# Winograd products of a gated FFN on one NeuronCore: another order of the second-level stages, and the last add and product of three units in four moved into the next unit

## The chip, the cores and the metric

The kernel runs on one core of one Trainium2 chip. The metric is the device time of one execution in microseconds. The engines are TensorE (PE; PEld for its weight loads), VectorE (DVE), ScalarE (ACT), GpSimd (POOL) and SyncE (SP). Each works through its own instructions in order, and they wait for one another by semaphores. TensorE writes its products to banks of PSUM.

## The reference

x has 4096 rows (2 x 2048) of 512 float32 values. Everything is float32.

```
x = x + attention(layernorm(x))     # scores and softmax over features (512 x 512), per batch
n = layernorm(x)
gate = n @ lut[gate_idx].T          # 4096 x 1376
up   = n @ lut[up_idx].T            # 4096 x 1376
h = silu(gate) * up
out = x + h @ lut[down_idx].T       # 4096 x 512
```

The table lut has 16 values; the index matrices have 1376 x 512 entries (down_idx 512 x 1376).

## The kernel before

**Stages.** Up to about 290 us of the profile the kernel does the first layernorm, the attention and the second layernorm. Then come the gate and up products (to about 815 us), then the down product. While TensorE multiplies, VectorE turns indices into weights: for each block of 128 rows of a weight matrix a chain of bit operations and predicated copies (`Job.ops`, lines 261 to 296). These lookups are traced in small portions between the stages of a unit: `between()` calls `pump(pace)`, which traces lookup operations worth about `pace` us.

**Units.** The 1376 hidden features are 11 blocks f (0 to 10; the last has 96), the 4096 rows are 4 pairs p of two chunks of 512. A unit (f, p), class `GateUp`, multiplies one block's gate and up weights with one pair of chunks. Gate and up, and two halves of the 512 features, make a 2 x 2 block product in Winograd's form, with 7 products instead of 8. Each is a stage of a unit that works on PSUM banks a, b and c (two of each in turn):

- a1 ("11"): bank a. ScalarE copies it to p1 (bank b in role 0, SBUF else).
- c1 ("S3","T3"): bank c. ScalarE copies it to p7, and in roles 2 and 3 also to v.
- a2 ("S2","T2"): added onto bank a. ScalarE copies the sum to u2.
- c2 ("22","T4") and b ("12","21"): see below.
- a3 ("S1","T1"): added onto bank a. VectorE makes c22 = a + p7.
- a4 ("S4","22"): added onto bank a. ScalarE makes h1 = silu(a). This stage runs inside the next unit, and so does `end`: h1 *= c22, stored to DRAM.
- `first`: h0 *= u2, stored to DRAM, where h0 is the silu of what b gives.

**Second level.** For f = 2 to 9 the stages b and c2 are done by Winograd once more, over 2 x 2 units: blocks f, f+1 and pairs p, p+1. Two objects of class `Second` do it: `of_b` (bank x, one only) and `of_c` (bank z, one only). Of the eight single products that b (or c2) of four units would take, each object saves one. A unit's place in the group is its role: 0 (f even, p even), 1 (f even, p odd), 2 (f odd, p even), 3 (f odd, p odd). The order of units is (f,0) to (f,3), so roles run 0 1 0 1 and, a block later, 2 3 2 3. Counting single products of 128x128 weights with 128x512 values: role 0 has 14, role 1 has 16, role 2 has 14, role 3 has 10 (no b and no c2 at all).

Role 1 makes "parts": after the products (S2,T2) and (S1,T1) of each object, ScalarE copies the bank (`part`, "r6" and "r5"), and SyncE stores the copy to DRAM; the object's next product is added onto the same bank and so waits for the copy. Role 2 adds a further product onto r5 by an accumulating DMA from GpSimd. Roles 2 and 3 get their parts back by accumulating DMAs from GpSimd onto p1 (for b) and v (for c2): `add_part`. So in role 2: u2 += z, u2 += v, h0 = x + p1; in role 3 u2 += v, h0 = silu(p1).

**The order that is written out.** `Line.run` (lines 1139 to 1162 before the change) traces one unit: a1, extra0, c1, extra1, the last unit's a4, a2, extra2, c2, the last unit's `end`, then b and a3 (a3 and b in the very last), then `first`; a `between()` stands behind each stage. The engines' queues follow this order exactly. `loads` (line 984) issues, ahead of a unit, the reloads of the right-hand sums T1, T2, T4 that the unit after it needs, on SyncE. `sums_left` makes the left sums S1 to S4 of both objects (tiles lb, lc; 4 operations each of 128x128).

In the profile, a product's operation has the line of `mm` (L998), with the bank as output: `a_g`, `b_g`, `c_g`, `x_g`, `z_g`. Adds have L136, subtractions L133; ScalarE's copies: p1 L1035, p7 L1050, v L1053, u2 L1059, parts L944; silu h0 L1109, silu h1 L1127; h0 * u2 L1119, h1 * c22 L1130. Buffer numbers are left out of names, so p1 and p7 both show as `p`, h0 and h1 as `h`.

Of the kernel before, what the change touches and what calls it, by code (L numbers as in the profile page):

```python
# [67 lines left out]
def tile_attn_ffn(  # L68
# [66 lines left out]
    def add(dest, a, b):  # L135
        nc.vector.tensor_tensor(dest, a, b, ALU.add)  # L136


    class Norm:
# [32 lines left out]
        def first(self, block):  # L172

            self.xn = xnp.tile([P, KB, 2, P], F32, tag="xn", name=f"xn_{self.name}_0", bufs=2)
            x = block.rearrange("p (i e) -> p i e", i=KB)
            half = KB // 2
            self.rest(0, 1, lambda: nc.vector.tensor_scalar(  # L177
                self.xn[:, half:, 0, :], x[:, half:, :], self.mv[:, 0, 0:1], self.rstd[:, 0:1],
                ALU.subtract, ALU.mult,
            ))  # L180
            nc.scalar.activation(
                self.xn[:, :half, 0, :], x[:, :half, :], AF.Identity,
                bias=self.nmr[:, 0:1], scale=self.rstd[:, 0:1],
            )
# [200 lines left out]
    def step():  # L385

        while deferred and deferred[0][0]():
            cost = next(deferred[0][1], None)
            if cost is not None:
                return cost  # L390
            deferred.pop(0)
        return next(lookup, None)
# [76 lines left out]
    def left(t, name, order=("S2", "S4", "S1")):  # L469
        a11, a21 = t[:, 0:2, :H], t[:, 0:2, H:]  # L470
        a12, a22 = t[:, 2:4, :H], t[:, 2:4, H:]

        def s3():
            for tag in order:
                o.new(tag)
            sub(a21, a11, a21)
            o.update({"11": a11, "12": a12, "22": a22, "S3": a21})

        o = Operand(name, [
            s3, lambda: sub(o["S2"], a22, a21), lambda: sub(o["S4"], a12, o["S2"]),  # L480
            lambda: add(o["S1"], o["S2"], a11),
        ])
        return o
# [111 lines left out]
    class Square:  # L595
# [7 lines left out]
        def mm(self, ps, a, b, first):  # L603
            for m in range(2):
                for k in range(2):

                    nc.tensor.matmul(  # L607
                        ps[:, m, :], self.a[a][:, k, m * P : (m + 1) * P], self.b[b][:, k, :],
                        start=first and m == k == 0, stop=k == 1,
                        skip_group_check=not (first and m == 0),  # L610
                    )
# [23 lines left out]
        def c2(self):  # L635
            self.mm(self.v, "22", "T4", False)
            add(self.c21, self.v, self.c21)
# [54 lines left out]
    g = [g_ops[0], left(gs[1], "g_1")]  # L692
# [186 lines left out]
    class Second:  # L879
# [34 lines left out]
        def sums_left(self, f):  # L914

            pool = wgu if self is of_b else x2p
            t = pool.tile([P, 4, P], F32, tag=f"l{self.name}", name=f"l{self.name}_{f}", bufs=1)
            (a11, a12), (a21, a22) = self.weights(f), self.weights(f + 1)
            s1, s2, s3, s4 = (t[:, q, :] for q in range(4))
            self.left = {"22": a22, "S1": s1, "S2": s2, "S3": s3, "S4": s4}  # L920
            return [
                lambda: add(s1, a21, a22), lambda: sub(s2, s1, a11),
                lambda: sub(s3, a11, a21), lambda: sub(s4, a12, s2),
            ]
# [33 lines left out]
    def in_two(t):  # L958
        return t[:, 0, :], t[:, 1, :]

    of_b = Second("b", "x", lambda f: in_two(gw[f][:, 2:4, :]), lambda p: in_two(xs[p]["21"]))
    of_c = Second("c", "z", lambda f: in_two(uw[f][:, 2:4, :]), lambda p: in_two(xs[p]["T4"]))
    seconds = [of_b, of_c]

    def there(f):
        return f in gw and len(gw[f].shape) == 3 and f in uw
# [17 lines left out]
    def loads(f, p):  # L984

        g = p // 2
        if 1 < f < NFT - 1 and f % 2 == 0 and p % 2:
            for tag in ("T2", "T1"):
                for o in (of_c, of_b):
                    o.load(g, tag)  # L990
        elif 1 < f < NFT - 1 and f % 2 and p % 2 == 0:
            for o in (of_c, of_b):
                o.load(g, "T4")
# [9 lines left out]
    class GateUp:  # L1003
# [57 lines left out]
        def c2(self):  # L1061
            if self.role is None:
                mm(self.c, self.pairs("22", "T4"), False)
                add(self.u2, self.c, self.u2)
            elif self.role == 0:
                of_c.begin(self, "11", "11")
                mm(self.c, of_c.pair(self, "12", "21"), False)
                add(self.u2, of_c.ps, self.u2)
                add(self.u2, self.c, self.u2)
            elif self.role == 1:  # L1070
                add(self.u2, self.c, self.u2)
                of_c.go_on(self, "S4", "22")
                add(self.u2, of_c.ps, self.u2)
            elif self.role == 2:
                of_c.go_on(self, "22", "T4")
                add(self.u2, of_c.ps, self.u2)
                add(self.u2, self.v, self.u2)

        def extra1(self):
            if self.role == 1:  # L1080
                of_c.go_on(self, "S1", "T1")
                of_c.part(self, "r5")
                of_b.go_on(self, "S2", "T2")
                of_b.part(self, "r6")
            elif self.role == 2:
                of_b.begin(self, "S3", "T3")
                of_b.part(self, "r5", onto=True)

        def extra2(self):
            if self.role == 1:  # L1090
                of_b.go_on(self, "S1", "T1")
                of_b.part(self, "r5")
# [21 lines left out]
            add(self.c22, self.a, self.p7)  # L1114

        def first(self):
            if self.role == 3:
                add(self.u2, self.v, self.u2)
            nc.vector.tensor_tensor(self.h0, self.h0, self.u2, ALU.mult)  # L1119
            self.store(self.h0, 2 * self.p)  # L1120
# [12 lines left out]
    class Line:  # L1133
# [3 lines left out]
            self.last, self.between = None, between  # L1137

        def run(self, u, final=False):
            u.a1()  # L1140
            self.between()
            u.extra0()
            u.c1()
            self.between()
            u.extra1()
            last, self.last = self.last, u
            if last is not None:
                last.a4()
                self.between()
            u.a2()  # L1150
            self.between()
            u.extra2()
            u.c2()
            if last is not None:
                last.end()
            self.between()
            one, two = (u.a3, u.b) if final else (u.b, u.a3)
            one()
            self.between()
            two()  # L1160
            u.first()
            self.between()

        def flush(self):
# [4 lines left out]
    pace = [1.0]  # L1169
# [93 lines left out]
    class Down:  # L1263
# [92 lines left out]
        def first(self):  # L1356
            pass

        extra0 = extra1 = extra2 = first

        def end(self):
            pass
# [3 lines left out]
    def by_two(ops):  # L1366
        return [
            lambda v=ops[i : i + 2]: [op() for op in v] for i in range(0, len(ops), 2)
        ]
# [5 lines left out]
    for (f, p), following in zip(units, units[1:] + [(NFT, 0)]):  # L1375
        while f not in gu or 1 < f < NFT - 1 and p and not there(f | 1):
            step()
        assert p in xs
        if 1 < f < NFT - 1 and f % 2 == 0 and p == 0:
            sums_of.append(f)  # L1380
        elif sums_of:
            for op in sums_left(sums_of.pop()):
                op()
        if f == NFT - 1 and p == 0:
            assert not todo and next(lookup, None) is None
            x2p.release()
            gub.release()
            for name in ("hp0", "dT"):
                hps[name] = tc.alloc_tile_pool(
                    name=name, bufs=1, side="right", reuse_waits="tile"  # L1390
                )
            hps[0] = hps["hp0"]
            h = Hidden(0)
            todo += by_two(sums_last(f) + down_sums(hps["dT"]))
        if f == NFT - 1 and p == 1:
            h.rest_of()
            todo += by_two(h.sums())
        if f == NFT - 1 and p == 3:
            units = [Down(h, 0)]
        loads(*following)  # L1400
        u = GateUp(f, p)
        pace[0] = {1: 1.2, 3: 0.8}.get(u.role, 1.07)
        line.run(u, final=(f, p) == (NFT - 1, NPR - 1))
        if p == NPR - 1:
            passed[0] = f + 1
        if (f, p) == (1, 1):
            xnp.release()
            x2p = tc.alloc_tile_pool(name="x2p", bufs=1, side="right", reuse_waits="tile")
        if f == 1 and p % 2:
            todo += by_two([op for o in seconds for op in o.sums(p // 2)])  # L1410
# [6 lines left out]
    for c in range(NCH):  # L1417
        nxt = None
        for jj in range(2):
# [10 lines left out]
            u = units.pop(0)  # L1430
# [64 lines left out]
```

## Time and profile before

| | us |
|---|---|
| median of 3 runs | 1091.05 |
| lowest, highest | 1088.09, 1091.49 |
| profiled execution | 1090.39 |
| its span | 1088.6 |
| TensorE busy | 1072.0 |
| VectorE busy | 768.7 |
| ScalarE busy | 360.4 |
| GpSimd busy | 79.7 |

The span is from the first to the last instruction of the profiled execution; its own time is 1.8 us more. TensorE's records overlap: two products in a row on one bank show as four records (each float32 product as two) of together 1.88 us, and the next stage starts 1.72 us after them. A number in brackets behind a row is the time that the engine stood idle before it, with what ended it. Row names hold engine, line, operation, output and inputs, shape and count.

### The profile page before, as it was taken

The numbers are of one execution on the slowest core, as the hardware profiler recorded it, in microseconds if no ns is written. First come the engines' busy times: TensorE is split into PE (matmuls) and PEld (weight loads), VectorE is DVE, ScalarE is ACT, GpSimd is POOL, SyncE is SP. The second block draws the span as 40 slices with busy tenths as digits, with TensorE's granted clock in tenths as the row PEclk, the third lists the DMA queues.
The fourth block names the chain that finished last, engine by engine and source line by source line (L and its number), as shares of the span: only waits on it lengthen the run. The fifth ranks groups of instructions, "written<-read, shape, count | busy, mean of one in ns | idle before, by whom it ended". The sixth has DMA issues, their size and how long they took to land.

```text
span 1088.6 us, 10783 instructions
## 1 busy us (share of the span) xinstructions
PE 1072.0 (98%) x3426; PEld 640.0 (59%) x3426; DVE 768.7 (71%) x1660; ACT 360.4 (33%) x671; POOL 79.7 (7%) x118
## 2 busy tenths in 40 slices
PE   9999999999999999999999999999999999999998
PEld 5668886444444444444434443444338888888887
DVE  7888777889885988898888888887543334433341
ACT  4652522554622233433443343333221111111110
POOL 0000000012110000310120031012000000000000
PEclk9999999999999999999999999999999999999999
DMA  8750314598651354653573466356515544345521
GB/s 343 227 164 22 76 40 97 141 226 215 175 142 39 118 181 155 156 144 136 145 161 131 163 143 148 130 144 143 158 53 172 172 152 156 98 148 178 156 68 39
DMA packets 107769, 153.89 MB, mean 141 GB/s; under 512 B 16432, under 2 KB 52528, under 8 KB 106816
## 3 DMA queue, kind: packets, MB, share of 16 engines
q1 hardware_dynamic: 75744, 107.51, 30.6%
q0 software_dynamic: 11904, 28.91, 13.4%
q10 hardware_dynamic: 20064, 16.78, 4.8%
q8 instruction: 27, 0.44, 0.2%
q14 instruction: 30, 0.25, 0.1%
HBM read 89.73 MB, written 63.44 MB: 141 GB/s over the span
## 4 chain that ended last, share of the span: by engine, by line
PE 86%; DVE 4%; DMA 4%; issue 3%; ACT 2%; POOL 1%; ACTq 0%; SPq 0%; POOLq 0%; DVEq 0%
PE a_g L998 22%; PE a_d L998 14%; PE y L770 10%; PE c_g L998 8%; PE c_d L998 7%; PE gp L454 4%; PE b_d L998 4%; PE z_g L998 3%; PE x_g L998 3%; PE b_g L998 3%; DMA v<-part_r_c 2%; PE ea_t L607 1%; PE ea_p L607 1%; PE ea_m L607 1%; DMA hd<-h 1%
## 5 line engine op out<-in xcount | busy, mean ns | idle before, releaser
L770 PE MATMUL y<-m,nT 128*128 128x512 f32 x256 | 110.2, 592 | 0.0
L998 PE MATMUL a_g<-xb,s 128*128 128x512 f32 (+1 forms) x176 | 83.2, 595 | 3.3 <-DVE c L136 3.3
L998 PE MATMUL a_g<-xT_a,s 128*128 128x512 f32 (+1 forms) x176 | 83.1, 594 | 2.7 <-ACT u L1059 2.7
L770 PEld LDWEIGHTS y<-m,nT 128*128 128x128 f32 x256 | 48.6, 190 | 60.4 <-issue 57.4
L998 PE MATMUL a_g<-xb,wg 128*128 128x512 f32 (+1 forms) x176 | 82.7, 592 | 0.0
L998 PE MATMUL c_g<-xb,wu 128*128 128x512 f32 (+1 forms) x176 | 82.7, 592 | 0.0
L454 PE MATMUL gp<-xn_a 128*128 128x128 f32 (+3 forms) x256 | 70.1, 434 | 1.5 <-DVE xn_a L177 1.2
L998 PE MATMUL a_g<-xT_sq,s 128*128 128x512 f32 (+1 forms) x132 | 62.4, 595 | 2.7 <-ACT u L1059 2.7
L998 PEld LDWEIGHTS a_g<-xb,s 128*128 128x128 f32 (+1 forms) x176 | 32.6, 187 | 47.6 <-issue 35.3
L454 PEld LDWEIGHTS gp<-xn_a 128*128 128x128 f32 x256 | 43.9, 190 | 28.3 <-issue 15.1
L998 PEld LDWEIGHTS a_g<-xT_a,s 128*128 128x128 f32 (+1 forms) x176 | 32.7, 187 | 46.6 <-issue 39.9
L998 PEld LDWEIGHTS c_g<-xb,wu 128*128 128x128 f32 (+1 forms) x176 | 33.0, 188 | 42.5 <-issue 42.3
L998 PEld LDWEIGHTS a_g<-xb,wg 128*128 128x128 f32 (+1 forms) x176 | 33.0, 188 | 42.5 <-issue 42.3
L290 DVE COPY_PREDICATED wd<-b_wd,wd 128x512 f32<-128x512 int16 (+1 forms) x77 | 56.5, 734 | 1.9
L998 PE MATMUL a_d<-dT,hs_a 128*128 128x256 f32 x224 | 56.2, 378 | 0.0
L136 DVE TENSOR_TENSOR u<-c_g,u 128x512 f32<-128x512 f32 (+1 forms) x28 | 19.3, 690 | 46.9 <-PE c_g L998 31.7
L136 DVE TENSOR_TENSOR r<-r,a_d 128x256 f32<-128x256 f32 x32 | 13.5, 421 | 53.7 <-PE a_d L998 53.7
L998 PEld LDWEIGHTS a_d<-dT,hs_a 128*128 128x128 f32 x224 | 42.4, 189 | 6.0
L998 PEld LDWEIGHTS a_g<-xT_sq,s 128*128 128x128 f32 (+1 forms) x132 | 24.4, 187 | 36.0 <-issue 29.5
L278 DVE TENSOR_SCALAR wd<-idx_wd,lut_x,lut_sb 128x512 int32<-128x512 int32 (+1 forms) x88 | 45.0, 540 | 0.0
L1109 ACT ACTIVATE h<-h 128x512 f32<-128x512 f32 x24 | 15.1, 631 | 84.8 <-DVE h L136 84.8
L1059 ACT COPY u<-a_g 128x512 f32<-128x512 f32 (+1 forms) x44 | 25.7, 585 | 46.7 <-PE a_g L998 42.8
(316 smaller groups left out, 2033.4 us busy)
## 6 DMA issues: line engine op xcount, KB each, us to landing
hd<-h SPq DMA_DIRECT2D x80, 256.0 KB, 2.0
h<-hd SPq DMA_DIRECT2D x40, 512.0 KB, 6.7
nl<-nd SPq DMA_DIRECT2D x32, 256.0 KB, 5.8
xnd<-xn_f ACTq DMA_DIRECT2D x16, 512.0 KB, 6.0
fl<-xnd POOLq DMA_DIRECT2D x32, 256.0 KB, 6.6
xn_back<-xnd SPq DMA_DIRECT2D x32, 256.0 KB, 4.2
out_dram<-r SPq DMA_DIRECT2D x31, 256.0 KB, 2.9
x<-in_x_dram SPq DMA_DIRECT2D x7, 1024.0 KB, 13.8
```

Source lines behind the costliest of these rows:

```text
L136: nc.vector.tensor_tensor(dest, a, b, ALU.add)
L278: vec.tensor_scalar(dest.bitcast(I32), idx, lut_x[:rows, k : k + 1], lut_i[:rows, at : at + 1], ALU.bitwise_and, ALU.bitwise_xor,)
L290: vec.copy_predicated(dest, masks[level - 1], t)
L454: nc.tensor.matmul(gp[b][i][:, i * P :], xn[:, i, j % 2, :], xn[:, i:, j % 2, :], start=c % CPB == 0 and j == 0, stop=c % CPB == CPB - 1 a ...
L607: nc.tensor.matmul(ps[:, m, :], self.a[a][:, k, m * P : (m + 1) * P], self.b[b][:, k, :], start=first and m == k == 0, stop=k == 1, skip_g ...
L770: nc.tensor.matmul(ys[k], nTs[k][:, i, :], m[:, i, :], start=(i == 0), stop=(i == KB - 1))
L998: nc.tensor.matmul(ps, lhsT, rhs, start=first and i == 0, stop=i == len(pairs) - 1, skip_group_check=not first,)
L1059: nc.scalar.copy(self.u2, self.a)
L1109: nc.scalar.activation(h0, self.p1 if self.role in (None, 3) else h0, AF.Silu)
```

## The change

1. Second-level stages of role 1: x of (S2,T2) goes from behind c1 (`extra1`) to behind a2 (`extra2`); x of (S1,T1) goes from there to behind c2 (a new `extra3`); a3 comes ahead of b in roles 1 and 3.
2. Role 3: the a4 of the unit before goes from ahead of a2 to behind a2.
3. Roles 1, 2 and 3: `first` (h0 *= u2 and the store) is traced in the next unit, behind its a1. The add u2 += v of role 2 goes there too (role 3 had it in `first` already).
4. `seconds` lists of_c ahead of of_b, so right-hand sums and left sums are made for c first; `loads` takes T2 and T1 of c, then T2 and T1 of b.
5. The paces are 1.3, 1.03 and 0.75 for roles 1, 2, 3 (before 1.2, 1.07, 0.8); role 0 and all others keep 1.07.

```diff
-    seconds = [of_b, of_c]
+    seconds = [of_c, of_b]
...
-            for tag in ("T2", "T1"):
-                for o in (of_c, of_b):
-                    o.load(g, tag)
+            of_c.load(g, "T2", "T1")
+            of_b.load(g, "T2", "T1")
...
                 add(self.u2, of_c.ps, self.u2)
-                add(self.u2, self.v, self.u2)
...
                 of_c.go_on(self, "S1", "T1")
                 of_c.part(self, "r5")
-                of_b.go_on(self, "S2", "T2")
-                of_b.part(self, "r6")
...
         def extra2(self):
+            if self.role == 1:
+                of_b.go_on(self, "S2", "T2")
+                of_b.part(self, "r6")
+
+        def extra3(self):
             if self.role == 1:
                 of_b.go_on(self, "S1", "T1")
                 of_b.part(self, "r5")
...
         def first(self):
-            if self.role == 3:
+            if self.role in (2, 3):
                 add(self.u2, self.v, self.u2)
...
         def run(self, u, final=False):
+            last, self.last = self.last, u
+
+            def last_a4():
+                if last is not None:
+                    last.a4()
+                    self.between()
+
+            role = getattr(u, "role", None)
             u.a1()
             self.between()
+            if getattr(last, "role", None):
+                last.first()
             u.extra0()
             u.c1()
             self.between()
             u.extra1()
-            last, self.last = self.last, u
-            if last is not None:
-                last.a4()
-                self.between()
+            if role != 3:
+                last_a4()
             u.a2()
             self.between()
+            if role == 3:
+                last_a4()
             u.extra2()
             u.c2()
             if last is not None:
                 last.end()
             self.between()
-            one, two = (u.a3, u.b) if final else (u.b, u.a3)
+            u.extra3()
+            one, two = (u.a3, u.b) if final or role in (1, 3) else (u.b, u.a3)
             one()
             self.between()
             two()
-            u.first()
+            if not role:
+                u.first()
             self.between()
...
-        pace[0] = {1: 1.2, 3: 0.8}.get(u.role, 1.07)
+        pace[0] = {1: 1.3, 2: 1.03, 3: 0.75}.get(u.role, 1.07)
```

More of the change, by code (lines that the diff above doesn't have):

```diff
@@ L1357, in first @@
             pass
-        extra0 = extra1 = extra2 = first
+        extra0 = extra1 = extra2 = extra3 = first
         def end(self):
```

## The prediction

> **What bounds the kernel now.** I read the page first, then TensorE's waits, then its timeline from 376 to 812 us, then VectorE, ScalarE and GpSimd (POOL) beside the places where TensorE stood. The page's first row:
>
> ```profile
> PE 1072.0 (98%) x3426; PEld 640.0 (59%) x3426; DVE 768.7 (71%) x1660; ACT 360.4 (33%) x671; POOL 79.7 (7%) x118
> ```
>
> The granted clock is full in every slice, so time can only be saved where TensorE stands still. The view of TensorE's waits names three kinds in the stage that is edited; all others lie before 130 us and are not touched:
>
> ```profile
> PE a_g L998 <- ACT u L1059: 5.4, 8, 0.7
> PE a_g L998 <- DVE c L136: 3.3, 4, 1.5
> PE z_g L998 <- DVE lc L133: 1.2, 1, 1.2
> ```
>
> A wait's number leaves out the tail and the restart, so I price waits by start to start. The edited stage (f = 2 to 9) runs from the a1 of unit (2,0) at 380.43 to the a1 of (10,0) at 765.54: 385.1 us. Eight groups of four units hold 14 + 16 + 14 + 10 = 54 products (unit kinds, "roles", 0 to 3), 432 in all. An undisturbed stage of two products takes 1.717 us start to start (443.89 to 445.61 below), so 432 need 370.9. **14.2 us are lost here**, and that is all that reordering can win. Where they go, in TensorE's timeline at a role-3 unit, (3,1):
>
> ```profile
> 443.89 1.88 PE L998 MATMUL a_g<-xT_sq,s 128*128 128x512 f32 x4
> 445.61 1.88 PE L998 MATMUL a_g<-xb,wg 128*128 128x512 f32 x4
> 447.32 1.88 PE L998 MATMUL c_g<-xb,wu 128*128 128x512 f32 x4
> 449.79 1.98 PE L998 MATMUL a_g<-xb,s 128*128 128x512 f32 x4 [0.58 <-DVE c L136]
> 451.61 1.88 PE L998 MATMUL a_g<-xT_a,s 128*128 128x512 f32 x4
> 454.16 1.98 PE L998 MATMUL a_g<-xT_a,s 128*128 128x512 f32 x4 [0.68 <-ACT u L1059]
> 455.98 1.88 PE L998 MATMUL a_g<-xb,wg 128*128 128x512 f32 x4
> ```
>
> The rows are a3 of role 2, then a1, c1, the a4 that belongs to role 2, a2, a3 of role 3, and the next a1. (i) a3 adds onto the bank that ScalarE must first copy out after a2, and role 3 has no product between: from 451.61 to 455.98 are 4.37 us for 3.43. 0.94 each, eight times: **7.5**. (ii) a4 adds onto the bank of role 2, which VectorE reads as c22; where that read is late a4 waits: 0.85 here, and by the same reckoning 0.22 at 544.76, 0.59 at 566.89, 1.18 at 641.29, 1.75 at 664.59: **4.6**. (iii) z at 395.50, once: **1.4**. (iv) **0.7**: eight times 0.08 in role 1. The sum is 14.2.
>
> Why c22 is late stands in VectorE's timeline:
>
> ```profile
> 443.30 0.69 DVE L136 TENSOR_TENSOR u<-z_g,u 128x512 f32<-128x512 f32 x1 [1.19 <-PE z_g L998]
> 445.05 0.69 DVE L136 TENSOR_TENSOR u<-v,u 128x512 f32<-128x512 f32 x1 [1.06 <-DMA v<-part_r_c]
> ...
> 447.33 0.69 DVE L136 TENSOR_TENSOR h<-x_g,p 128x512 f32<-128x512 f32 x1
> ...
> 449.05 0.69 DVE L136 TENSOR_TENSOR c<-a_g,p 128x512 f32<-128x512 f32 x1
> 449.65 0.68 DVE L1119 TENSOR_TENSOR h<-h,u 128x512 f32<-128x512 f32 x1
> ```
>
> VectorE works in order. u2 += v waits for a DMA that adds a part onto v, and h0 (h<-x_g) and c22 (c<-a_g) queue behind it.
>
> **The change, part by part.** No instruction is added or taken away on any engine; all of it is order.
>
> *a4 of role 2 goes behind a2 of role 3.* The 1.72 us of a4 then lie between a2 and a3, where ScalarE's copy costs 0.94: (i) goes, 7.5. a4 itself comes 1.72 us later, and the greatest lateness was 1.75; with the next part (ii) goes too, 4.6. What is late next: a3 now follows a4 at once, and the next unit's a1 takes the bank of a4, so ScalarE must finish silu(h1) within a3's 1.72 us; the product's tail of 0.16 and 0.60 for the silu (451.81) leave 0.9. a2 now follows c1 at once and needs the p1 copy (0.57) within c1: ScalarE made it 0.6 us late at 448.59 only because it sat behind silu(h0), which waited for the h0 add; that comes 1.1 us earlier below.
>
> *u2 += v and h0 * u2 of roles 1 to 3 go into the next unit behind a1; role 2's add no longer stands ahead of h0 and c22.* VectorE's wait for v in role 2 (1.06 here, up to 1.89 at 659.78) is gone: v landed from 0.5 us before to 0.3 us after the start of role 3, and the add now comes 3 to 4 us after it. The new wait: ScalarE's copy into v in role 3 needs this add, and behind that copy queue the u2 copy (which a3 needs) and silu(h1). From the rows of the tightest unit, role 2 at 647.49 and role 3 at 659.50: z add at 657.20, then h1 * c22 (0.60), two COPY_PREDICATED (1.4), h0 (0.60), two TENSOR_SCALAR (0.9), c22 (0.60), and three lookups (1.7 to 2.2), by the order of the changed program: the add begins 4.1 and ends 4.7 us behind role 3's a1. The v copy (0.59) then ends at 5.3 to 5.4, the u2 copy (0.58) at 6.0, and a3 is due at 6.9. In (7,1), where a cast of 0.5 stands between the copies, 6.5. No loss, with 0.4 to 0.9 us in hand. The price beyond that is one for one.
>
> Role 3's own add and product run in the next unit. The v DMA takes 5.5 us (3.9 to 6.7) and lands 10.6 to 11.8 behind role 3's a1; VectorE gets there at about 11 to 12. It may still stand 1 us, as now (0.48 at 457.50); c22 is already read, and the next v copy is due at 13.5. On SyncE the h0 store moves behind the next unit's loads, which so leave earlier; h0's buffer is written again some 9.5 us into that unit, and the store (2.0 us) ends by 6 or 7.
>
> *Role 1: x of (S2,T2) behind a2, x of (S1,T1) behind c2, a3 ahead of b.* Now one z product lies between the two x products, while ScalarE copies the part out. The same gap is there now, between (S1,T1) and (S4,22), in the timeline of the unit at 489.54:
>
> ```profile
> 498.99 1.02 PE L998 MATMUL x_g<-T_b_in,lb 128*128 128x512 f32 x2
> 499.84 1.02 PE L998 MATMUL z_g<-xT_a,lc 128*128 128x512 f32 x2
> 500.70 1.10 PE L998 MATMUL x_g<-xb,lb 128*128 128x512 f32 x2
> ```
>
> It costs the 0.08 of (iv). The old gap is filled by a3, the new one takes its place: (iv) stays, with bounds of -0.7 (both hidden) and +4 (a cast of 0.5 ahead of the copy, eight times; in the changed order none stands there). POOL and SyncE issue the same DMAs; the parts made in role 1 are read three units on, and r5 goes out behind an h1 store at no cost.
>
> *c before b in the left sums and the loads.* The lc sum that z at 395.50 waits for moves ahead of four lb operations (393.90 to 394.83): up to 0.93. But the next z needs the part's copy, which ScalarE ran at 397.49 to 398.08 behind a silu that waited for VectorE, and that z starts at 398.18, with or without the first. I take 0, with 0.93 as the other end. The loads only swap T1 of c with T2 of b, issued about 12 us ahead of use.
>
> *Pace.* 1.07 + 1.2 + 1.07 + 0.8 becomes 1.07 + 1.3 + 1.03 + 0.75: the lookups keep their rate. VectorE was 87 to 89% busy from 400 to 700 us; the same work in 373 instead of 385 us is about 91%, so it does not become the bound on the mean.
>
> **Sum.** 1090.39 (profiled execution: span 1088.6 and 1.8 around it) - 7.5 - 4.6 = **1078.3**. The median of the runs is 1091.05, 0.7 above, and they spread from 1088.09 to 1091.49. Below about 0.3% (3.3 us) a measurement of this kernel can't be told from no change.
>
> **The rivals.**
>
> *VectorE's lateness comes back through ScalarE.* The deferred add passes 4.8 us behind role 3's a1 in the crowded units, and the v copy holds the u2 copy. For it: 0.4 us of slack in (7,1), and a busier VectorE. Against it: its waits for z (1.0 to 1.5 in role 2) show that it catches up each unit. 7.5 saved, 4.6 given back elsewhere: 1082.9.
>
> *Role 3 is too short.* With a2 right behind c1 and a1 right behind a3, either waits as a3 did: 0.94 x 8 back, only 4.6 saved: 1085.8. Against it: 0.9 us of slack at the silu.
>
> *Nothing comes of it.* Both happen: 1090.4.
>
> *Slower: v lands late.* One place: the add of role 2's v, in role 3. TensorE loses once the add begins more than 4.8 us behind role 3's a1, that is, if v lands 4.5 us later than any did. At 7.0 in all eight units it would cost 8 x 2.2 = 17.6: 1095.9. For it: these DMAs are issued by POOL beside a VectorE that gets denser. Against it: POOL's issue of them took 861 to 1127 ns (median 870) at 89% VectorE busy, and the landings spread by only 2.8 us. The Trainium skill ("SBUF — State Buffer", "Who interferes with whom" and the box on SWDGE ahead of it) says that descriptors of POOL's DMAs wait while VectorE holds the port that both share, so by that rule denser work delays v. The issue times show at most a quarter of a microsecond of this, far from 4.5.
>
> **How the numbers follow.** The forecast 0.70, lateness through ScalarE 0.12, role 3 too short 0.06, nothing 0.07, slower 0.05. Faster by over 0.3% is the first three: 0.88. The range takes in the first two (0.82): below, 1078.3 - 0.9 - 0.7 and the 1 us by which runs differ, 1075.5; above, 1082.9 and the same, 1084.5.
>
> **What would show it.** Right: in TensorE's waits the eight "ACT u" are gone and the rows "DVE c" too; a role-3 unit takes 8.6 us from a1 to a1; (2,0) to (10,0) takes 373 us. VectorE's waits for v fall to those of role 3. Wrong: "ACT u" stays, now at an a3 behind a4, with the v copy late (rival one); a wait at a1 or a2 of or behind role 3 (rival two); v landing later than 7 us behind its issue (the slower one). The stages before 380 and behind 766 us should not change.

## The result, and the profile after

| | before | after |
|---|---|---|
| median of the runs, us | 1090.24 (4 runs, 1088.09 to 1091.49) | 1078.94 (4 runs, 1078.82 to 1079.50) |
| profiled execution, us | 1090.39 | 1078.93 |
| its span | 1088.6 | 1077.2 |
| TensorE from the a1 of (2,0) to the a1 of (10,0) | 380.43 to 765.54 = 385.11 | 380.47 to 754.09 = 373.62 |

The time after is 0.9899 of the time before, with a 95% interval from 0.9882 to 0.9917. Of the two profiled executions, the changed one is 11.46 us shorter, and its edited stage is 11.49 us shorter: outside that stage the two agree to 0.03 us in sum.

Lines from here on are those of the changed kernel (`mm` is L997, u2 copy L1058, v copy L1052, p1 copy L1034, silu of h1 L1128); kernels made from the one before keep its numbers (L998, L1059), and a run that adds or drops a line shifts them. The first row of the page of the changed kernel, and TensorE's waits in it from 380 to 770 us (sum, times, longest):

```profile
PE 1068.6 (99%) x3426; PEld 641.0 (60%) x3426; DVE 768.0 (71%) x1660; ACT 360.5 (33%) x671; POOL 79.7 (7%) x118
```

```profile
PE z_g L997 <- DVE lc L133: 0.9, 1, 0.9
PE z_g L997 <- ACT r_c L944: 0.7, 1, 0.7
```

The instruction counts are the same as before. The eight waits for the u2 copy and the four for c22 are gone, and the two rows that are left lie in one unit, the first of role 1. TensorE's timeline of the changed kernel at the role-3 unit (3,1):

```profile
444.58 1.88 PE L997 MATMUL a_g<-xT_sq,s 128*128 128x512 f32 x4
446.30 1.88 PE L997 MATMUL a_g<-xb,wg 128*128 128x512 f32 x4
448.01 1.88 PE L997 MATMUL c_g<-xb,wu 128*128 128x512 f32 x4
449.73 1.88 PE L997 MATMUL a_g<-xT_a,s 128*128 128x512 f32 x4
451.45 1.88 PE L997 MATMUL a_g<-xb,s 128*128 128x512 f32 x4
453.17 1.88 PE L997 MATMUL a_g<-xT_a,s 128*128 128x512 f32 x4
454.88 1.88 PE L997 MATMUL a_g<-xb,wg 128*128 128x512 f32 x4
```

Each stage starts 1.72 us behind the last, with no bracket. From a1 to a1 are 8.58 us, and a4 of role 2 (451.45) stands between a2 and a3. VectorE and then ScalarE beside it:

```profile
446.32 0.68 DVE L136 TENSOR_TENSOR h<-x_g,p 128x512 f32<-128x512 f32 x1
...
447.99 0.68 DVE L136 TENSOR_TENSOR c<-a_g,p 128x512 f32<-128x512 f32 x1
...
450.56 0.68 DVE L136 TENSOR_TENSOR u<-v,u 128x512 f32<-128x512 f32 x1
451.34 0.69 DVE L1120 TENSOR_TENSOR h<-h,u 128x512 f32<-128x512 f32 x1
```

```profile
448.21 0.59 ACT L1034 COPY p<-a_g 128x512 f32<-128x512 f32 x1 [0.55 <-PE a_g L997]
...
451.27 0.59 ACT L1052 COPY v<-c_g 128x512 f32<-128x512 f32 x1 [0.71 <-DVE u L136]
451.75 0.62 ACT L252 CAST b_u<-idx_u 128x512 int16<-128x512 int32 x1
452.27 0.59 ACT L1058 COPY u<-a_g 128x512 f32<-128x512 f32 x1
```

The adds to h0 and c22 now come first and wait for nothing. The deferred u2 += v begins 4.26 us behind a1. The v copy waits for it, a cast and the u2 copy follow, and that ends at 6.56, with a3 due at 6.87. The p1 copy here waits for TensorE alone.

By start to start, 2.8 us remain lost of 14.2: z in the first role-1 unit 2.14, and eight gaps of 0.08.

### The profile page after: what moved, and what is told of

The parts are those of the page before. It is cut to its first block, busy times and chain, and to the rows that moved or that the text cites. A ratio compares the mean times of both kernels' runs of the same rounds, so it can differ in the third digit from the quotient of the medians.

```text
span 1077.2 us, 10786 instructions
## 1 busy us (share of the span) xinstructions
PE 1068.6 (99%) x3426; PEld 641.0 (60%) x3426; DVE 768.0 (71%) x1660; ACT 360.5 (33%) x671; POOL 79.7 (7%) x118
## 4 chain that ended last, share of the span: by engine, by line
PE 90%; DVE 4%; ACT 2%; DMA 1%; issue 1%; ACTq 1%; SPq 0%; DVEq 0%
PE a_g L997 27%; PE a_d L997 14%; PE y L770 10%; PE c_g L997 9%; PE c_d L997 7%; PE b_d L997 4%; PE x_g L997 4%; PE z_g L997 4%; PE b_g L997 2%; PE ea_t L607 1%; PE ea_p L607 1%; PE ea_m L607 1%; DVE st_a L154 1%; PE gp L454 1%; DMA x<-in_x_dram 1%
## 5 line engine op out<-in xcount | busy, mean ns | idle before, releaser
L997 PE MATMUL a_g<-xb,s 128*128 128x512 f32 (+1 forms) x176 | 82.7, 592 | 0.0
L997 PE MATMUL a_g<-xb,wg 128*128 128x512 f32 (+1 forms) x176 | 82.7, 592 | 0.0
L997 PE MATMUL c_g<-xb,wu 128*128 128x512 f32 (+1 forms) x176 | 82.7, 592 | 0.0
L997 PE MATMUL a_g<-xT_a,s 128*128 128x512 f32 (+1 forms) x176 | 82.7, 592 | 0.0
L997 PE MATMUL a_g<-xT_sq,s 128*128 128x512 f32 (+1 forms) x132 | 62.0, 592 | 0.0
L997 PEld LDWEIGHTS a_g<-xb,s 128*128 128x128 f32 (+1 forms) x176 | 33.0, 188 | 42.5 <-issue 39.6
L997 PEld LDWEIGHTS a_g<-xT_a,s 128*128 128x128 f32 (+1 forms) x176 | 33.0, 188 | 42.5 <-issue 41.8
L997 PEld LDWEIGHTS c_g<-xb,wu 128*128 128x128 f32 (+1 forms) x176 | 33.0, 188 | 42.5 <-issue 42.3
L997 PEld LDWEIGHTS a_g<-xb,wg 128*128 128x128 f32 (+1 forms) x176 | 33.0, 188 | 42.5 <-issue 42.3
L997 PE MATMUL a_d<-dT,hs_a 128*128 128x256 f32 x224 | 56.2, 379 | 0.0
L997 PEld LDWEIGHTS a_d<-dT,hs_a 128*128 128x128 f32 x224 | 42.4, 189 | 6.0
L997 PEld LDWEIGHTS a_g<-xT_sq,s 128*128 128x128 f32 (+1 forms) x132 | 24.8, 188 | 31.9 <-issue 31.4
L1128 ACT ACTIVATE h<-a_g 128x512 f32<-128x512 f32 (+1 forms) x44 | 26.2, 597 | 43.9 <-PE a_g L997 43.9
```

The costliest lines, as they stand in the source:

```text
L997: nc.tensor.matmul(ps, lhsT, rhs, start=first and i == 0, stop=i == len(pairs) - 1, skip_group_check=not first,)
L1128: nc.scalar.activation(self.h1, self.a, AF.Silu)
```

## Experiments

The theory: (i) goes because a4 of role 2 covers the u2 copy; (ii) goes because a4 moves, and because VectorE no longer holds c22 and the p1 copy behind v; what is left is z. Rivals are named at each run. "Excess" is start to start less 1.717 us for two products, from each kernel's profiled execution. A ratio is to runs of the kernel before that were made beside the experiment (medians 1089.82 to 1090.42), with its 95% interval in square brackets.

**a4 back ahead of a2, the rest of the change kept.** In `run`:

```
-            if role != 3:
-                last_a4()
+            last_a4()
             u.a2()
             self.between()
-            if role == 3:
-                last_a4()
```

> The whole change but one part: the a4 of the unit before stays ahead of a2 in role 3. The theory (the a4 behind a2 is what hides ScalarE's copy ahead of a3) expects the eight waits of 0.94 us back and nothing else: 1078.9 + 7.5 = 1086.4 us, eight rows 'ACT u' of 0.68 us in TensorE's waits, and no row 'DVE c', since VectorE's read of c22 is no longer behind the wait for v. The rival, that a4 waits for c22 again as soon as it comes 1.72 us earlier, expects 1088 to 1091.

Measured 1086.76 (8 runs, 1084.93 to 1087.66), 0.9971 of before [0.9959, 0.9982]. TensorE's waits of this kernel:

```profile
PE a_g L997 <- ACT u L1058: 5.4, 8, 0.7
```

The row of before is back with all eight, at 0.7 each, and there is none for c22. The place of a4 alone is worth the 7.5 us of (i); without it the other edits still remove (ii).

**a4 behind a2 in role 3, nothing else changed from before.**

```
-            if last is not None:
-                last.a4()
-                self.between()
+            if role != 3:
+                last_a4()
             u.a2()
             self.between()
+            if role == 3:
+                last_a4()
```

> The kernel before with one part of the change: the a4 behind a2 in role 3. The theory: the eight waits of a3 (7.5 us) and the waits of a4 (4.6 us) both go, but a2 now follows c1 at once and needs the p1 copy, which ScalarE makes late behind a silu that waits for VectorE, which waits for v. By the rows of before, where p1 was copied 0.1 us (3,1), 0.6 us (7,1) and 2.0 us (7,3) behind the place of the new a2, some 3 us of waits at a2: 1081 to 1082 us. The rival, that the moved add of v brings nothing once a4 is moved, expects 1078.3.

Measured 1083.48 (3 runs, 1081.79 to 1084.36), 0.9934 [0.9903, 0.9965]. Its TensorE, VectorE and ScalarE at (3,1), whose a1 starts at 446.60:

```profile
448.32 1.88 PE L998 MATMUL c_g<-xb,wu 128*128 128x512 f32 x4
451.58 1.98 PE L998 MATMUL a_g<-xT_a,s 128*128 128x512 f32 x4 [1.38 <-ACT p L1035]
```

```profile
447.42 0.69 DVE L136 TENSOR_TENSOR u<-v,u 128x512 f32<-128x512 f32 x1 [2.43 <-DMA v<-part_r_c]
...
449.70 0.68 DVE L136 TENSOR_TENSOR h<-x_g,p 128x512 f32<-128x512 f32 x1
```

```profile
450.42 0.63 ACT L1109 ACTIVATE h<-h 128x512 f32<-128x512 f32 x1 [6.47 <-DVE h L136]
450.96 0.57 ACT L1035 COPY p<-a_g 128x512 f32<-128x512 f32 x1
```

To be read from below: a2 adds onto the bank that the p1 copy reads; the copy sits behind silu(h0); silu waits for the h0 add; that one is queued behind u2 += v, which waited 2.43 us for a DMA. No wait for the u2 copy or c22 is left, but a2 now loses 1.64 here and 5.1 in five of the eight units. So moving a4 alone saves (i) and (ii) and gives back 5.1, where about 3 was expected; z, too, lost 2.83 in this execution instead of 1.48. The deferral is what takes the p1 copy off that chain.

**The deferral alone, nothing else changed from before.** The add goes from `c2` of role 2 to `first`, and `first` of roles 1 to 3 goes behind the next unit's a1:

```
-                add(self.u2, self.v, self.u2)
...
-            if self.role == 3:
+            if self.role in (2, 3):
                 add(self.u2, self.v, self.u2)
...
             u.a1()
             self.between()
+            if getattr(last, "role", None):
+                last.first()
...
-            u.first()
+            if not getattr(u, "role", None):
+                u.first()
```

> The kernel before with one part of the change: u2 += v and h0 * u2 of roles 1 to 3 in the next unit. The theory expects the waits of a4 for c22 to go (4.6 us) and the eight of a3 to stay (7.5 us): 1085.8 us, no row 'DVE c', eight rows 'ACT u' of 0.68 us. The rival, that c22 is late because VectorE is busy and not because it waits for v, expects most of the 4.6 us to stay: 1088 to 1091.

Measured 1086.61 (7 runs, 1086.14 to 1086.86), 0.9971 [0.9959, 0.9983]. The waits for c22 are gone and all eight for the u2 copy stand (5.4 us in its row, as before). The deferral by itself is worth (ii); of the 0.8 us over the expectation 0.45 are z's (1.93 here, 1.48 before), and 0.4 lie outside the edited stage, which takes 380.96 us instead of 385.11.

**The x products of role 1 where they were**, a3 ahead of b kept: (S2,T2) of `of_b` goes from `extra2` back to `extra1`, (S1,T1) from `extra3` to `extra2`.

> The changed kernel, with the x products of role 1 where they were ((S2,T2) behind c1, (S1,T1) behind a2) and a3 ahead of b kept. Then a4 and a2, or z and a3, lie between any two x products. The theory expects the eight gaps of 0.08 us to go and nothing else to move: 0.7 us, 1078.2. The rival, that the new places of the x products carried a part of the gain, expects 1079.5 to 1082.

Measured 1078.19 (4 runs, 1077.31 to 1078.46), 0.9887 [0.9871, 0.9904]. The eight gaps of 0.08 are gone, and z lost 1.59 instead of 2.14. But a new wait of 0.34, 0.45 with its restart, stands at (7,1), where the add begins at 4.86. VectorE's row shows why:

```profile
631.70 0.69 DVE L136 TENSOR_TENSOR h<-x_g,p 128x512 f32<-128x512 f32 x1 [0.70 <-DMA hd<-h]
```

h0 of role 2 is written into the one buffer of h0, and the store of role 1's h0 had not landed. With (S2,T2) ahead of role 1's a2 again, VectorE reaches h0 * u2 0.9 us later; the store left 5.94 us ahead of the a1 of (7,1) instead of 6.89, and landed 0.48 behind it instead of 2.07 ahead. So the moved x products cost the 0.7 us of (iv), by the gaps that went, and kept this store out of the way. The 0.7 us between the two medians fit the expectation, but by the traces three terms add up to it: 0.67 of gaps and 0.55 of z gained, 0.45 lost.

**`of_b` ahead of `of_c` in the list again:** `seconds = [of_b, of_c]`.

> The changed kernel, with of_b ahead of of_c in the list again (the loads stay c first). The changed kernel lost 2.1 us at the two z products of the first unit of role 1, the kernel before 1.4 (one wait, and 0.05). The theory: VectorE's T sums stand still until a store to DRAM has freed their buffer, 3.6 us with c first and 2.9 with b first, and that sets both. It expects about 1.4 us here: 1078.2. The rival, that the order of c and b decides by its four operations, expects the first z wait to be 0.9 us longer than in the changed kernel: 1079.8.

Measured 1078.96 (4 runs, 1078.42 to 1081.29), 0.9900 [0.9886, 0.9915]. The profiled execution was the slowest, 1081.29; the other three lie beside the changed kernel's, so the times do not tell the two orders apart. In the profiled one 4.42 us are lost around the two z products, but not all of it by waiting. The granted clock was 0.5 from 397.39 to 400.80 us, while TensorE was busy, and full in the rest of the stage; the c1 between the two z's took 3.12 us instead of 1.88:

```profile
398.31 3.12 PE L997 MATMUL c_g<-xb,wu 128*128 128x512 f32 x4
```

3.41 us at half the clock cost 1.71; the waits lost the other 2.71. Beside the wait of VectorE's T sums for stores, in each execution with the three shared buffers:

| list | T sums wait, us | the two z's lose, us |
|---|---|---|
| c first (changed kernel 3.55) | 2.61, 2.75, 3.00, 3.55, 3.78 | 1.19, 1.34, 1.59, 2.14, 2.37 |
| b first (kernel before 2.88, this run 4.22) | 2.88, 3.35, 4.22, 4.28 | 1.48, 1.93, 2.71, 2.83 |

In both orders the loss is the wait less 1.4 to 1.5. So the theory's "that sets both" holds, but its 3.6 us for c first and 2.9 for b first were one execution each and not a property of the order. For the same wait, c first makes the first z lose 0.93 less and the second 0.93 more: the order is worth nothing.

**The store that z waits for.** The right sums T1, T2, T4 are made in three rotating buffers ("rt") and stored to DRAM; a fourth sum waits until the first is stored. Here those of `of_b`'s second pair get buffers that are free by then:

```
-                r[tag] = x2p.tile([P, CH], F32, tag="rt", name=f"{tag}_{self.name}{g}", bufs=3)
+                at, bufs = ("tt", 7) if self is of_b and g == 1 else ("rt", 3)
+                r[tag] = x2p.tile([P, CH], F32, tag=at, name=f"{tag}_{self.name}{g}", bufs=bufs)
```

> The changed kernel, with the T sums of b of the second pair of units in three buffers that are free at that time (those of the reloads), so that VectorE need not wait there for a store. The theory (the wait for the store sets the z products of the first unit of role 1) expects both z waits to go, 2.1 us: 1076.8. The rival, that the lc sums and the silu are late by VectorE's other work, expects at least 1 us to stay: 1078 or more.

Measured 1076.64 (4 runs, 1076.55 to 1076.93), 0.9875 [0.9861, 0.9890]. TensorE's timeline in the first role-1 unit, of the changed kernel and then of this one:

```profile
395.26 1.12 PE L997 MATMUL z_g<-T_c_in,lc 128*128 128x512 f32 x2 [0.90 <-DVE lc L133]
396.22 1.88 PE L997 MATMUL c_g<-xb,wu 128*128 128x512 f32 x4
398.82 1.13 PE L997 MATMUL z_g<-T_c_in,lc 128*128 128x512 f32 x2 [0.72 <-ACT r_c L944]
```

```profile
393.94 1.02 PE L998 MATMUL z_g<-T_c_in,lc 128*128 128x512 f32 x2
394.80 1.88 PE L998 MATMUL c_g<-xb,wu 128*128 128x512 f32 x4
396.52 1.02 PE L998 MATMUL z_g<-T_c_in,lc 128*128 128x512 f32 x2
```

Both brackets are gone, and the time falls by 2.3 us, about the 2.14 of z. The z wait comes from the three shared buffers, and so from the store that one of them waits for.

**The price of a late add, in two strengths.** Lookups are asked for ahead of the deferred add in role 3; the rate of role 3 is lowered to 0.6 (0.4 in the stronger):

```
             u.a1()
             self.between()
+            if role == 3:
+                pump(1.0)        # 2.5 in the stronger
             if getattr(last, "role", None):
                 last.first()
```

> The changed kernel, with 1 us more of lookups on VectorE ahead of the moved add in role 3 (and the pace of role 3 lowered from 0.75 to 0.6, so that the lookups keep about their rate). In the changed kernel the u2 copy ends 6.1 to 6.6 us behind role 3's a1 in the crowded units and a3 is due at 6.9. The theory of a slack of 0.3 to 0.8 us and a price of one for one beyond it expects the copy 1.0 to 1.4 us later, and so waits of a3 for 'ACT u' of 0.2 to 0.9 us in five or six of the eight units: 2 to 5 us, 1081 to 1084 us. The rival, that ScalarE's v copy is not on the path, expects 1078.9.

Measured 1079.48 (2 runs, 1078.68 and 1080.29), 0.9906 [0.9877, 0.9935]. The add moved by only 0.5 to 1.2 us in seven units, to begin at 4.2 to 4.85. The u2 copy ended at up to 7.00, and a3 was late in five units by 0.04 to 0.18 us (1.1 in all with the restarts). The 2 to 5 us that were expected did not come, and two runs are too few to tell the theories apart by time.

> The changed kernel, with 2.5 us of lookups asked for ahead of the deferred add in role 3 (the rate of role 3 lowered to 0.4, so that the lookups of a group stay about the same): 3 to 7 VectorE instructions more stand ahead of the add in seven of the eight role-3 units, some 0.57 us each. Theory (one for one beyond 4.8 us): the add begins at 5.5 to 6.8 us behind role 3's a1 in these seven, a3 waits for ScalarE's u2 copy by 0.8 to 2.0 us and 0.1 of restart in each, about 10 us in all, so 1087 to 1091. Rival (ScalarE's chain of add, v copy and u2 copy does not end on TensorE's path, and the small loss of the milder version was chance): no wait named for the u2 copy, 1079. Second rival (VectorE has idle time ahead of the add that takes up the lookups): the add begins below 5.3 us, under 3 us lost, 1080 to 1082.

Measured 1088.88 (10 runs, 1088.09 to 1090.22), 0.9981 [0.9971, 0.9990]. Its waits for the u2 copy, and ScalarE and TensorE at (3,1), whose a1 starts at 447.21:

```profile
PE a_g L997 <- ACT u L1058: 8.4, 7, 1.5
```

```profile
454.28 0.58 ACT L1052 COPY v<-c_g 128x512 f32<-128x512 f32 x1 [2.81 <-DVE u L136]
455.13 0.59 ACT L1058 COPY u<-a_g 128x512 f32<-128x512 f32 x1 [0.27 <-DVE h L1120]
```

```profile
455.77 1.55 PE L997 MATMUL a_g<-xT_a,s 128*128 128x512 f32 x3 [1.53 <-ACT u L1058]
```

In seven units the add begins at 5.7 to 6.4, and a3 is late in just these seven: 9.5 us, and 0.7 of restarts. In the six of them without a cast between the copies, a3 starts 2.14 to 2.21 us behind the start of the add. Added to 1078.94 the 10.2 us give 1089.1, and the median is 1088.88. The profiled execution itself took 1090.22: its edited stage is 9.45 longer than the changed kernel's (10.2, less 0.8 that z lost less), and the granted clock was 0.5 for 3.41 us from 7.89 us on, which cost 1.7 ahead of the stage. The chain from the add to a3 is on the path, and its price is one for one. The second bracket shows a link that the prediction did not have: the u2 copy also waits for h0 * u2, which reads the buffer that it writes.

**The best parts together:** the x products back and the free rooms.

> The changed kernel with both: x products of role 1 where they were, and free buffers for the T sums of b. If the two losses that are left (0.7 and 2.1 us) are as read, nothing is lost any more from the a1 of (2,0) to the a1 of (10,0): 370.9 us, and the time is 1078.9 - 2.8 = 1076.1. The rival, that they share a cause or that the next wait lies right behind, expects 1077 to 1079.

Measured 1076.19 (4 runs, 1076.03 to 1076.68), 0.9871 [0.9857, 0.9886]. One wait is left in the profiled execution, which was the slowest: 0.38 and a restart of 0.10 at (3,1), where the add began at 4.89. As in the run with the x products back, VectorE's add to h0 had waited for the h0 store there, by 0.55.

**And the deferred add ahead of the lookups behind a1, in role 3:**

```
             u.a1()
+            if role == 3:
+                last.first()
             self.between()
-            if getattr(last, "role", None):
+            if role != 3 and getattr(last, "role", None):
                 last.first()
```

> The last version (parts of x where they were, sums of b for the second pair in other rooms), and in role 3 the deferred add and product of role 2 stand directly behind a1, ahead of the lookups that follow a1: one lookup of 0.45 to 0.7 us fewer is queued ahead of the add. Theory (TensorE pays one for one for what the add begins beyond 4.8 us behind role 3's a1): the add, at 4.89 us in the crowded unit (3,1) of the last version, begins at about 4.2 to 4.4, ScalarE's u2 copy ends at 6.5 to 6.7, the wait of 0.38 with its restart of 0.10 there goes, and the time is 1075.7 (the last version measured 1076.19 median). No wait of TensorE is left between 380 and 766 us. Rival (the wait in (3,1) comes from the cast that stands between ScalarE's copies and not from the add): the wait stays and the time is 1076.2.

Measured 1076.27 (4 runs, 1076.24 to 1076.43), 0.9868 [0.9853, 0.9883]. In (3,1) the add begins at 3.49 and the u2 copy ends at 5.94, although the cast still stands there (4.68 to 5.30); the wait is gone, so it was the add's. The add came 1.4 us earlier, of which the edit explains 0.8: the h0 store landed 0.26 ahead of the add to h0, so that this one did not wait. No gap over 0.05 us is left, and from the a1 of (2,0) to that of (10,0) are 370.8 us. The time did not fall to 1075.7, though: that was reckoned from the median of the version before, whose profiled execution, the one with the wait, lay 0.5 above it. That is the 370.9 of an undisturbed stage: reordering can give no more in this stage.

## Why the prediction was right, point by point

**(i), 7.5 us: as said.** Gone in the changed kernel, back with a4 in its old place.

**(ii), 4.6 us: as said.** Either edit alone removes it. But the prediction's "a2 needs the p1 copy within c1", with the 1.1 us by which the h0 add comes earlier, turned out to be the reason that both are needed: with a4 moved alone, a2 pays 5.1. In the changed kernel the eight p1 copies begin 1.92 to 2.05 us behind a1 and a2 is due at 3.43. (The copy at 448.59 in the kernel before began 2.98 behind a1, so it was 1.06 late by this measure, not 0.6.)

**The new wait, ScalarE's v copy in role 3: no loss, as said; the slack was overrated by a little.** Forecast: the add begins at 4.1 us, the u2 copy ends at 6.0, or 6.5 with a cast. Measured in the eight units: 0.81 to 4.26, then 5.9 to 6.56. The add may begin no later than about 4.66 (6.87 less 2.21), not 4.8, since h0 * u2 stands between add and u2 copy; where a cast stands between the copies, a3 began 2.35 behind the add in three runs, and so no later than about 4.52. In the profiled execution of the changed kernel 0.3 us were in hand at the tightest place, (3,1), which has such a cast; (7,3), which the prediction took for the tightest, began its add at 3.92.

**z, taken as 0 out of 0 to 0.93: the order was worth the 0, and the term that was mis-sized is the wait behind it.** z's loss grew from 1.48 to 2.14, past both bounds. The lc sum moved ahead of four operations as expected, and the next z gave the 0.93 back as expected. But VectorE's T sums, ahead of both, wait for a store, and the prediction held that wait fixed. VectorE's wait in the kernel before, and then in the changed one:

```profile
388.69 0.69 DVE L133 TENSOR_TENSOR T_c<-xT_x,xT_sq 128x512 f32<-128x512 f32 x1 [2.88 <-DMA far_b1T<-T_b]
```

```profile
389.39 0.69 DVE L133 TENSOR_TENSOR T_b<-xb,xb 128x512 f32<-128x512 f32 x1 [3.55 <-DMA far_c1T<-T_c]
```

The store left 3.85 us behind the a1 of (2,0) in both and landed 5.05 us later instead of 4.37. These 0.67 us are the 0.66 by which z lost more, and the second z began at 398.82 and not at the 398.18 that the prediction gave it. Where it lands in one execution is luck as far as these runs go (see the last section), so the prediction's distance of 0.6 us from the result is, too. With the measured terms 1090.39 - 7.5 - 4.6 + 0.66 = 1078.95, and 1078.93 was measured.

**(iv), 0.7: stays, as said.** Eight gaps of 0.08, now at x's (S1,T1).

**The h0 store: later than reckoned, at no cost in the changed kernel.** The prediction let the store end 6 or 7 us into the next unit, ahead of a write at 9.5. In the changed kernel's units of role 0 it landed at 6.5 to 8.9, and the write came at 9.6. In role 3, where ScalarE's silu writes the buffer from 7.6 us on, it landed at 7.7 to 10.3 in seven of the eight units, and the silu stood for it by up to 2.67 us; TensorE did not wait for that silu. In role 2 VectorE's add to h0 waited for this store in two experiments, and there a3 lost 0.45 and 0.49 us.

**The range.** Its ends, 1075.5 and 1084.5, are 0.2 and 0.6 us wider than the terms named for them give (1075.7 and 1083.9); 1078.94 lies inside either way.

**The rivals.** ScalarE's chain as a way to lose is real: the stronger of the two late adds makes 10 us of it. It did not occur because the add was in time. A role 3 too short showed nowhere in the changed kernel, only with a4 moved alone. v landed as early as before: from issue to landing 4.0, 5.2 and 6.8 us (lowest, median, highest) against 3.9, 5.5 and 6.7, and POOL's issue took 866 to 1094 ns against 861 to 1127. VectorE was busy 92% of the time from 400 to 700 us instead of 88%, and it was left with no wait for v at all. The rule of the Trainium skill that the prediction names ("SBUF — State Buffer", "Who interferes with whom") has the port held by certain kinds of VectorE operation only. Which of this kernel's operations are of those kinds no run here shows, so these figures do not test the rule.

## What to carry to other kernels

Where TensorE adds onto a bank that another engine must first read, count the products that lie between, and move one there from a neighbouring unit; then follow each queue to see what the move makes due earlier. An in-order engine that waits for a transfer delays everything queued behind it, through other engines too: put the consumer where the transfer has long landed, not where its result first could be used. When an edit is to be priced, find the point from which lateness counts one for one, and include the reader of every buffer that is written again, a store too.

## What the runs showed that was not expected

One store's landing moves from execution to execution. The store that the T sums wait for left 3.85 us behind the a1 of (2,0) in every profiled execution. The changed kernel, the one with a4 back and the two with a late add are the same program up to there, and it landed 5.05, 5.28, 4.11 and 4.25 us later. Over all nine kernels with the shared buffers z lost between 1.19 and 2.83 us. With other buffers it lost nothing, and the runs lay within 0.2 to 0.7 us of each other, against 3.4 us for the four of the kernel before. That this wait, once in a kernel of 1.08 ms, makes the spread of the runs is not shown: only one execution of each kernel has a trace, and the four runs of the changed kernel lie within 0.7 us with the wait in place. A second cause is in the traces: in two of the twelve the granted clock was 0.5 for 3.41 us between the first products and the last, which cost 1.7 us each time, and both were the slowest run of their kernel (1081.29 against 1078.42 to 1079.21, and 1090.22 against 1088.09 to 1089.27). TensorE had stood for 2.46 us just ahead of the one stretch and for 1.90 ahead of the other; in the run with a4 alone it stood for 2.52 us, and the clock stayed full. What moves the store, and what halves the clock, stays open.
